# A Swin block and a dynamic convolution: scores on four 64x64 tiles, the first norm a round ahead on VectorE, activation tables called ahead, the end of the round reordered

## The chip, the cores and the metric

The kernel runs on one core of a Trainium2 chip, in one launch. The metric is the device time of that core in microseconds (us), as the median of several executions. All data are float32.

The engines that matter are TensorE (PE, with its weight loads shown apart as PEld), VectorE (DVE), ScalarE (ACT), GpSimd (POOL) and SyncE (SP, used here only to issue DMAs). Each works through its own instructions in program order and waits for others by semaphores.

## The reference, cut to what matters

The input x has 16 images of 192 channels and 56x56 pixels. Layer 0 is a Swin block with windows of 7x7, shifted by 3; layer 1 is a 3x3 depthwise convolution whose weights are computed from the image itself. The gains are ones and the biases zeros, but the kernel doesn't rely on that.

```python
h   = LN(x over channels) * g1 + b1; roll by (-3, -3); cut into 8x8 windows of 49 tokens
qkv = h @ qkv_w + qkv_b                      # 6 heads of 32
a   = softmax(q * 32**-0.5 @ k.T + rel_bias + shift_mask)
x1  = x + roll_back(concat(a @ v) @ proj_w + proj_b)
y   = x1 + gelu(LN(x1) @ fc1_w + fc1_b) @ fc2_w + fc2_b        # 192 -> 768 -> 192

t   = relu(bn(mean(y over pixels) @ w1.T))                     # 192 -> 48
wt  = (t @ w2.T + b2) with the taps behind the centre set to 0 # 4 of 9 are left
out = depthwise_conv3x3(y, wt) + bias
```

## The kernel before

**Tiling.** Channels lie on partitions. An image stays in SBUF in two tiles: x0 holds channels 0 to 127 of all rows, x1 the other 64 channels of the upper half on partitions 0 to 63 and of the lower half on 64 to 127. A step i handles two rows of windows, one of each half (h = 0, 1): T = 392 tokens each, 784 together. An image has four steps, so there are NS = 64 steps. Three images are in SBUF at a time.

**The main loop** (from L794) is a software pipeline. One round i works on several steps at once: the statistics of the first norm for step i+1, the attention of step i, the second norm of step i-1, the MLP of step i-2. The order of instructions on each engine is the order of the program (`manual_schedule`), so it is written out by hand:

1. `norm_stats` (L345): products with a selection matrix give means and mean squares in PSUM tiles `st`. `norm_devs` (L359): ACT squares the mean, DVE subtracts, ACT takes the square root (L371), DVE the reciprocal (L372). `norm_spread` (L376): 16 small DMAs from SP spread the rows of `dev` over all partitions (`dv`).
2. `mlp_first` (L651): six blocks `ph` of 128 hidden channels in three PSUM pairs. Blocks 0 to 2 are finished first, by `long` products (128 channels) and `short` ones (64). The short products of blocks 3 to 5 need the banks that the Gelu of blocks 0 to 2 (L663, ACT) empties.
3. `norm1_scale` (L388): GpSimd multiplies x by `dv` and writes the windows `win` of step i+1.
4. `attention_scores` (L527): for each of four pairs of windows (`wp`) eight products `sc`, then on DVE the bias `e` (L556), the maximum `top` (L562), its subtraction (L563), on ACT the exponential (L566), on DVE the sum `tot` (L570) and its reciprocal, on GpSimd the product `prob` (L572). These stages are interleaved over the four pairs.
5. `mlp_second` (L679): products `pf1`, then `pf` for the six blocks; behind blocks 2 to 5 stands a turn of the attention, six transposes `pt` (L593) and their copy `prt` by ACT (L599). The turns alternate between two pairs of PSUM banks, so the third needs the first one's copy done.
6. `mlp_out` (DVE), then on GpSimd `norm_squares` of step i+2 and `norm2_scale` of step i-1, then `attention_values` (`po`), the rest of two convolutions, `attention_qk` (`pq`, `pk`, `pe`), `project` (`pp`), `attention_v` (`pv`) and its copies.

In the scores before, a product contracts over 128 partitions: `kbd` holds the keys as a block diagonal, four heads of 32 wide with zeros elsewhere. One product of 196 columns makes the scores of four heads for one window, and one of 98 columns those of two. Two windows run side by side, since their outputs lie on different halves of the PSUM partitions.

**Convolution.** When the last step of an image is done, `taps_pool`, `taps_first` and `taps_second` compute the four taps. Then six pieces of the image go through `conv_begin` (ACT, L746, tile `y`) and `conv_rest` (DVE, three taps at L761, then the DMA out), two pieces in each of three rounds. DVE's taps stand ahead of its four copies of the keys into `kbd` (L460). At the end of the program the six pieces of the last image come one after the other.

**Activation tables.** ACT holds one set of functions; Sqrt, Gelu and Exp lie in three sets. The compiler puts an ACT_TABLE_LOAD right ahead of the first ACTIVATE that needs another set, so three to a round. Copies, Square, Identity and Relu cause none in the trace.

**Loading.** `load_x` (L91) is issued from ACT at the top of round 4b-2, five DMAs for image b.

Of the kernel before, what the change touches and what calls it, by code (L numbers as in the profile page):

```python
# [8 lines left out]
F32 = mybir.dt.float32  # L9
AF = mybir.ActivationFunctionType  # L10
# [26 lines left out]
def tile_swin_then_dynamic_conv(  # L37
# [199 lines left out]

    rel_r = work.tile([PW, N, HEADS], F32, tag="y", name="rel_r")
    nc.vector.memset(rel_r, 0.0)
# [4 lines left out]
    for j in range(2):  # L244
        for yq in range(WS):
# [8 lines left out]
            )  # L254
    bias_t = const.tile([PW, 2, 2, HEADS, N], F32, tag="bias_t", name="bias_t")
    rel_hk = rel_r[:, ::-1, :].rearrange("p k h -> p h k")
    for r in range(2):
        for e in range(2):
            cut = mask_t[:, r, e, :].rearrange("p (o k) -> p o k", o=1)
            nc.vector.tensor_tensor(  # L260
                bias_t[:, r, e], rel_hk, cut.broadcast_to([PW, HEADS, N]), ALU.add
            )

# [41 lines left out]

    kbd = one.tile([128, 3, NWIN, 4, N], F32, tag="kbd", name="kbd")
    vbd = const.tile([128, 2, NWIN, HEADS // 2, 64], F32, tag="vbd", name="vbd")
# [22 lines left out]

    sqs, stats = {}, {}

    def norm_squares(key, i, side, engine):
# [25 lines left out]
    def norm_devs(keys):  # L359


        sides = sorted(keys)
        d = one.tile([128, T], F32, tag="dev", name=f"dev_{keys[sides[0]]}")
        mean = {s: slice(s * 64, s * 64 + 64) for s in sides}
        var = {s: slice(64 - s * 64, 128 - s * 64) for s in sides}
        for s in sides:
            nc.scalar.activation(d[var[s]], stats[s][mean[s], :T], AF.Square)
        for s in sides:
            nc.vector.tensor_tensor(d[var[s]], stats[s][var[s], :T], d[var[s]], ALU.subtract)
        p = slice(0, 128) if len(sides) == 2 else var[sides[0]]  # L370
        nc.scalar.activation(d[p], d[p], AF.Sqrt, bias=eps_t[p])  # L371
        nc.vector.reciprocal(d[p], d[p])  # L372
        stats.clear()
        return d

    def norm_spread(keys, d):  # L376

        out = {}
        for side in sorted(keys):
            v = one.tile([128, 2, T], F32, tag=f"sq0{side}", name=f"dv_{keys[side]}")  # L380
            for h in range(2):
                at = 64 - side * 64 + h * 32
                for p in range(0, 128, 32):
                    nc.sync.dma_start(v[p : p + 32, h], d[at : at + 32])
            out[side] = v
        return out

    def norm1_scale(i, dv):  # L388
# [6 lines left out]
        for ws, cs, at, n in (  # L395
# [9 lines left out]
            for h in range(2):  # L405
                nc.gpsimd.tensor_tensor(  # L406
                    w0[:, h, :, ws, cs],
                    wide(v0[:, h]).rearrange("p r (w c) -> p r w c", w=n),
                    wide(b4[:, h]).rearrange("p r (w c) -> p r w c", w=n),
                    ALU.mult,  # L410
                )
            for h in range(2):
                p = slice(h * 64, h * 64 + 64)
                nc.gpsimd.tensor_tensor(
                    w1_[p, :, ws, cs],
# [26 lines left out]
    def attention_qk(i):  # L442
# [4 lines left out]
        ps, dsts = [], []  # L447
        for name, k in (("q", 1), ("k", 2), ("e", 0)):
            p = banks(f"p{name}_{i}", k)
            ps.append(p)  # L450
            dsts.append([p[:, h, :T].rearrange("p (w t) -> p w t", t=N) for h in range(2)])
        for m in range(3):
            long(dsts[m], wqkv, slice(m * 128, (m + 1) * 128), r0, True)
        for m in range(3):
            short(dsts[m], wqkv, slice(m * 128, (m + 1) * 128), r1, False)
        pq, pk, pe = ps
        nc.scalar.activation(q4, pq[:, :, :T], AF.Identity, bias=qkb[:, 0:1])
        for h in range(4):
            p = slice(h * HD, (h + 1) * HD)
            nc.vector.tensor_scalar(  # L460
                kbd[p, 0:2, :, h, :],
                pk[p, :, :T].rearrange("p h (w t) -> p h w t", t=N),
# [4 lines left out]
        for a in range(2):  # L467
# [3 lines left out]
            for h in range(2):  # L471
                p = slice(64 + h * HD, 64 + (h + 1) * HD)
                g = a * 2 + h
                nc.scalar.activation(
                    kbd[g * HD : (g + 1) * HD, 2, :, g, :],
                    pe[p, a, :T].rearrange("p (w t) -> p w t", t=N),
# [5 lines left out]
    def attention_v(i):  # L482
# [20 lines left out]

        whole(0, True)
        rest(0, False)
        rest(1, True)
        whole(1, False)
        return pvs
# [18 lines left out]
    def attention_scores(i, q4, q2):  # L527
# [5 lines left out]
        def add(wp):  # L533
            sc = banks(f"sc_{i}_{wp}", (1, 2, 0, 1)[wp])
            for g in range(4):
                a, heads = g % 2, slice(0, 4 * N) if g < 2 else slice(4 * N, 6 * N)
                for s in range(2):
                    w = wp * 2 + s
                    m = 64 - s * (64 - N)
                    cols = slice(w * N, w * N + m)  # L540
                    if g < 2:
                        lhs, rhs = q4[:, a, cols], kbd[:, a, w]
                    else:
                        lhs, rhs = q2[:, cols], kbd[:, 2, w, 2 * a : 2 * a + 2]
                    mm(
                        sc[s * 64 : s * 64 + m, a, heads],
                        lhs,
                        rhs.rearrange("p h t -> p (h t)"),
                        True,
                        True,  # L550
                    )
            e = one.tile([PW, 2, HEADS * N], F32, tag="e", name=f"e_{i}_{wp}", bufs=4)
            rel = bias_t[:, :, int(wp == 3)].rearrange("p r h k -> p r (h k)")
            if not last:
                rel = rel[:, 0:1, :].broadcast_to([PW, 2, HEADS * N])
            nc.vector.tensor_tensor(e, sc[:PW, :, : HEADS * N], rel, ALU.add)  # L556
# [45 lines left out]
    def attention_weigh(po, po1, wp, prt):  # L602
        for s in range(2):
            w = wp * 2 + s
            for a, g in ((0, 0), (0, 1), (1, 0), (1, 1), (0, 2), (1, 2)):
                o = po[:, a] if g < 2 else po1
                at = (g if g < 2 else a) * 64
                mm(
                    o[at : at + 64, w * N : (w + 1) * N],
                    vbd[:, a, w, g, :],  # L610
                    prt[:, a, g * PW + s * 64 : g * PW + s * 64 + N],
                    True,
# [16 lines left out]
    def project(i, o):  # L629
        pp1, pp = bank(f"pp1_{i}", 0), banks(f"pp_{i}", 1)  # L630
        for a in range(2):
            p = slice(a * 64, a * 64 + 64)
            mm(pp[:, a, :T], wp1[p], o[p, 2], True, False)
        for a in range(2):
            mm(pp1[a * 64 : a * 64 + 64, :T], wp0[:, C0:DIM], o[:, a], True, False)
        mm(pp1[:, :T], wp2, o[:, 2], False, True)
        for a in range(2):
            mm(pp[:, a, :T], wp0[:, 0:C0], o[:, a], False, True)
        v0, v1 = rows_of(i)
# [102 lines left out]
    def conv_begin(b, wt, n):  # L742

        kc, lo = (0, n * PR) if n < 4 else (1, (n - 4) * PR)
        y = work.tile([128, PR, IMG], F32, tag="y", name=f"y_{b}_{n}")
        nc.scalar.activation(  # L746
# [39 lines left out]

    yns, convs, qs = {}, [], {}
    ctx.enter_context(tc.manual_schedule())

    def has(i):  # L790
        return 0 <= i < NS

    norm_squares("1_0", 0, 0, nc.gpsimd)
    for i in range(-1, NS + 2):  # L794
        if (i + 2) % STEPS == 0 and 0 < (i + 2) // STEPS < B:
            b = (i + 2) // STEPS
            images[b] = load_x(b, nc.scalar)
        keys = {}
        if has(i + 1):
            keys[0] = f"1_{i + 1}"  # L800
            norm_stats(keys[0], i + 1, 0)
        if has(i - 1):
            keys[1] = f"2_{i - 1}"
            norm_stats(keys[1], i - 1, 1)
        dvs = norm_spread(keys, norm_devs(keys)) if keys else {}

        taps = convs[-1] if convs and "pooled" in convs[-1] else None

        def first_tap():
            if taps:  # L810
                taps["tt"] = taps_first(taps["b"], taps.pop("pooled"))

        hid = None
        if has(i - 2):
            hid = one.tile([128, NFC, 2, T], F32, tag="hid", name=f"hid_{i - 2}")
            mlp_first(i - 2, yns.pop(i - 2), hid, first_tap)
        else:
            first_tap()
        if 0 in keys:
            norm1_scale(i + 1, dvs[0])  # L820
        if has(i):
            attention_scores(i, *qs.pop(i))
        ys = []
        if convs and "wt" in convs[0]:
            c = convs[0]
            ys = [(c, c["n"] + k, conv_begin(c["b"], c["wt"], c["n"] + k)) for k in range(2)]
        prts = []
# [7 lines left out]
        else:  # L835
            for wp in range(4):
                turn(wp)
        if has(i + 2):
            norm_squares(f"1_{i + 2}", i + 2, 0, nc.gpsimd)
        if 1 in keys:  # L840
            yns[i - 1] = norm2_scale(i - 1, dvs[1])
        o = attention_values(i, prts) if has(i) else None
        for c, n, y in ys:
            conv_rest(c["b"], c["wt"], n, y)
            c["n"] = n + 1
            if n == 5:
                convs.pop(0)
        if has(i + 1):
# [89 lines left out]
```

## Time and profile before

| | |
|---|---|
| time | 3599.22 us, median of 3 (3596.49 to 3600.29) |
| profiled span | 3594.4 us |
| first statistics product | 56.2 us |
| PE work in the scores | 270.6 us (sc) |
| PE work in the MLP | 838.0 us (ph) and 814.9 us (pf) |
| ACT table loads in the loop | 191, of 1283 ns each |
| GpSimd on the first norm | 181.2 us (L406) and 183.9 us (L414) |
| DVE on the convolution's taps | 387.5 us (L761), 1358 ns each |

The busy time of a group is its own; engines work side by side, so the numbers don't add up to the span. The mean of one PE product includes its way through the array, so products that follow each other overlap, and the pace has to be read from several in a row. The program's time is told by the chain that ended last; a wait of an engine that isn't on it costs nothing. Since rounds repeat closely, a single round, read as a timeline, tells most of it.

### The profile page before, as it was taken

How to read it: one execution, taken by the hardware profiler on the slowest of the kernel's cores; microseconds unless marked ns; L12 is line 12 of the kernel's file. 1: busy time of each engine (PE TensorE's matmuls, PEld its weight loads, DVE VectorE, ACT ScalarE, POOL GpSimd, SP SyncE). 2: the span in 40 equal slices, each digit the busy share in tenths (PEclk: the TensorE clock that was granted, in tenths of full speed). 3: DMA queues.
4: the chain of work that ended last, by engine and by line, in shares of the span. 5: the costliest groups of instructions: out<-in, count | busy, mean ns of one | idle time of the engine just before them, and what ended most of it. 6: DMA issues, size and time to landing. Idle time of an engine off the chain costs nothing.

```text
span 3594.4 us, 62190 instructions
## 1 busy us (share of the span) xinstructions
PE 3394.8 (94%) x24854; PEld 2031.3 (57%) x24854; DVE 2120.9 (59%) x3309; ACT 1723.9 (48%) x2675; POOL 1119.3 (31%) x1374
## 2 busy tenths in 40 slices
PE   4699999999999999999999999999999999999996
PEld 2455655555555555555655555555655655555553
DVE  2554566665755756666665755656666565656654
ACT  0344455454545455445444545445445445545542
POOL 2332332332332332332332332332332332332320
PEclk8799999999999999999999999999999999999998
DMA  2010102001010111102001010111112011010101
GB/s 61 14 46 19 37 28 62 21 28 55 28 55 28 32 42 37 46 28 63 19 28 55 28 55 28 44 30 36 46 32 59 19 33 50 28 55 28 29 22 49
DMA packets 83074, 135.12 MB, mean 38 GB/s; under 512 B 25537, under 2 KB 65890, under 8 KB 80738
## 3 DMA queue, kind: packets, MB, share of 16 engines
q1 hardware_dynamic: 68384, 92.52, 9.1%
q10 hardware_dynamic: 14402, 38.64, 3.7%
q8 instruction: 196, 3.21, 0.4%
q14 instruction: 92, 0.75, 0.1%
HBM read 41.15 MB, written 38.54 MB: 22 GB/s over the span
## 4 chain that ended last, share of the span: by engine, by line
PE 72%; DVE 16%; ACT 6%; issue 3%; ACTq 1%; DMA 1%; POOL 0%; SPq 0%; DVEq 0%; POOLq 0%
PE pf L89 21%; PE ph L89 19%; DVE y L761 9%; PE pv L89 8%; PE sc L89 7%; DVE kbd L460 5%; PE st L89 4%; PE pt L593 4%; PE pp L89 2%; ACT L663 2%; PE po L89 2%; ACT hid L663 2%; PE pq L89 1%; PE pk L89 1%; PE pe L89 1%
## 5 line engine op out<-in xcount | busy, mean ns | idle before, releaser
L89 PE MATMUL ph<-yn,wf 128*128 128x392 f32 (+1 forms) x3072 | 838.0, 512 | 69.3 <-ACT hid L663 69.3
L89 PE MATMUL pf<-hid,wf 128*64 128x392 f32 (+1 forms) x3072 | 814.9, 495 | 0.0
L406 POOL TENSOR_TENSOR win<-x,dv 128x343 f32<-128x343 f32 (+2 forms) x384 | 181.2, 486 | 1810.4 <-DMA dv<-dev 1512.6
L89 PEld LDWEIGHTS ph<-yn,wf 128*128 128x128 f32 (+1 forms) x3072 | 407.9, 187 | 490.7 <-ACT hid L663 173.9
L89 PEld LDWEIGHTS pf<-hid,wf 128*64 128x64 f32 (+1 forms) x3072 | 377.1, 163 | 304.2 <-issue 128.5
L556 DVE TENSOR_TENSOR e<-sc,bias_t 113x588 f32<-113x588 f32 x256 | 195.9, 766 | 597.4 <-PE sc L89 497.3
L572 POOL TENSOR_TENSOR prob<-e,tot 113x588 f32<-113x588 f32 x256 | 294.9, 1174 | 526.1 <-DVE tot L571 524.3
L663 ACT ACTIVATE hid<-ph,f1b 128x784 f32<-128x784 f32 x384 | 337.2, 913 | 208.3 <-PE ph L89 207.5
L761 DVE SCALAR_TENSOR_TENSOR y<-x,wt,y 128x770 f32<-128x770 f32 x288 | 387.5, 1358 | 9.2 <-ACT y L746 2.4
L460 DVE TENSOR_SCALAR kbd<-pk,qkb 32x784 f32<-32x784 f32 x256 | 263.8, 1030 | 204.0 <-PE pk L89 201.1
L566 ACT ACTIVATE e<-e 113x588 f32<-113x588 f32 x256 | 177.5, 693 | 300.9 <-DVE e L563 300.4
L89 PE MATMUL pv<-wqkv,win 64*128 64x192 f32 (+1 forms) x2048 | 292.1, 338 | 18.5 <-DVE kbd L460 18.3
L89 PEld LDWEIGHTS pv<-wqkv,win 64*128 64x128 f32 (+1 forms) x2048 | 248.2, 190 | 81.2 <-PE pp L89 43.5
L89 PE MATMUL sc<-kbd,q 128*64 128x196 f32 (+3 forms) x4096 | 270.6, 289 | 6.1 <-DVE e L556 6.1
L599 ACT COPY prt<-pt 128x678 f32<-128x678 f32 x256 | 182.3, 722 | 191.0 <-PE pt L593 190.8
L89 PEld LDWEIGHTS sc<-kbd,q 128*64 128x64 f32 (+1 forms) x4096 | 233.6, 130 | 66.6 <-ACT hid L663 34.6
L89 PE MATMUL pp<-o,wp 128*128 128x392 f32 (+2 forms) x896 | 249.4, 512 | 1.4 <-ACT o L623 1.4
L523 DVE COPY vbd<-pv 49x192 f32<-49x192 f32 x512 | 159.5, 350 | 142.6 <-ACT vbd L525 97.5
L563 DVE TENSOR_TENSOR e<-e,top 113x588 f32<-113x588 f32 x256 | 233.0, 910 | 8.9
L593 PEld LDWEIGHTS pt<-ident,prob 113*128 113x128 f32 x1536 | 169.4, 143 | 118.3 <-POOL prob L572 56.9
L372 DVE RECIPROCAL dev<-dev 128x392 f32<-128x392 f32 (+1 forms) x66 | 171.8, 2603 | 84.5 <-ACT dev L371 84.5
L593 PE MATMUL pt<-ident,prob 113*128 113x113 f32 x1536 | 197.8, 266 | 23.7 <-POOL prob L572 23.7
(114 smaller groups left out, 4240.8 us busy)
## 6 DMA issues: line engine op xcount, KB each, us to landing
dv<-dev SPq DMA_DIRECT2D x1024, 49.0 KB
x<-in_x_dram ACTq DMA_DIRECT2D x15, 1484.0 KB
out_dram<-y SPq DMA_DIRECT2D x48, 392.0 KB
out_dram<-y SPq DMA_DIRECT2D x48, 196.0 KB
x<-in_x_dram ACTq DMA_DIRECT2D x15, 392.0 KB
x<-in_x_dram ACTq DMA_DIRECT2D x15, 350.0 KB
out_dram<-y SPq DMA_DIRECT2D x16, 308.0 KB
out_dram<-y SPq DMA_DIRECT2D x16, 154.0 KB
```

Of the source, the lines that this page charges most:

```text
L89: nc.tensor.matmul(dst, lhs, rhs, start=start, stop=stop, skip_group_check=True)
L372: nc.vector.reciprocal(d[p], d[p])
L406: nc.gpsimd.tensor_tensor(w0[:, h, :, ws, cs], wide(v0[:, h]).rearrange("p r (w c) -> p r w c", w=n), wide(b4[:, h]).rearrange("p r (w c) ...
L460: nc.vector.tensor_scalar(kbd[p, 0:2, :, h, :], pk[p, :, :T].rearrange("p h (w t) -> p h w t", t=N), qkb[p, 1:2], None, ALU.add,)
L556: nc.vector.tensor_tensor(e, sc[:PW, :, : HEADS * N], rel, ALU.add)
L563: nc.vector.tensor_tensor(ehs[wp], ehs[wp], t.broadcast_to([PW, 2 * HEADS, N]), ALU.subtract)
L566: nc.scalar.activation(es[wp], es[wp], AF.Exp)
L572: nc.gpsimd.tensor_tensor(prob[wp][:PW, :, 0:N], ehs[wp], t.broadcast_to([PW, 2 * HEADS, N]), ALU.mult)
L593: nc.tensor.transpose(pt[:, a, g * PW : (g + 1) * PW], prob[wp][:PW, h : h + 2, :].rearrange("p h k -> p (h k)"), ident[:PW, :PW],)
L599: nc.scalar.copy(prt, pt[:, :, : 3 * PW])
L663: nc.scalar.activation(hid[:, f], phs[f][:, :, :T], AF.Gelu, bias=f1b[:, f : f + 1])
L761: nc.vector.scalar_tensor_tensor(dst, src, wt[:, kc, t : t + 1], dst, ALU.mult, ALU.add)
```

## The change

Four things are changed together.

- **Scores.** A product now contracts over 64 partitions, two heads wide (`kbd` has two heads side by side instead of four), and its 64 outputs lie on one half of the PSUM partitions. So it takes a 64x64 quarter of the array; four run side by side, of the two halves of partitions (r) and two windows (s). There are twelve products of 98 columns for a pair of windows. The two row halves write to different PSUM banks. The order of heads in `e`, `prob` and `bias_t` follows.
- **First norm.** Its statistics are taken for step i+2 and scaled one round later, for step i+1, on VectorE right behind the reciprocal. The loop starts a round earlier. `dv` of this side gets a tile of its own.
- **Tables.** A one-element ACTIVATE (`table`) calls for Gelu behind the square root, for Exp behind the first layer, for Sqrt behind the scores, so that the load stands there.
- **Order.** Convolutions run three to a round in two rounds instead of two in three, one of them inside `mlp_first`; `y` gets three buffers. The second norm goes ahead of the squares on GpSimd; keys are computed ahead of queries, and `project` and `attention_v` take their products in another order. Images are loaded from SP a round earlier.

```diff
-    bias_t = const.tile([PW, 2, 2, HEADS, N], F32, ...)       # 4 additions
+    bias_t = const.tile([PW, 2, 2, 2, HEADS * N], F32, ...)   # 24 additions of two heads
...
-    kbd = one.tile([128, 3, NWIN, 4, N], F32, tag="kbd", name="kbd")
+    kbd = one.tile([128, 3, NWIN, 2, N], F32, tag="kbd", name="kbd")
...
+    def table(func):
+        nc.scalar.activation(junk, eps_t[0:1], func)
...
         nc.scalar.activation(d[p], d[p], AF.Sqrt, bias=eps_t[p])
+        table(AF.Gelu)
         nc.vector.reciprocal(d[p], d[p])
...
-        for side in sorted(keys):
-            v = one.tile([128, 2, T], F32, tag=f"sq0{side}", name=f"dv_{keys[side]}")
+        for side in sorted(keys, reverse=True):
+            tag = ("dv1", "sq01")[side]
+            v = one.tile([128, 2, T], F32, tag=tag, name=f"dv_{keys[side]}")
...
-                nc.gpsimd.tensor_tensor(          # norm1_scale, both loops
+                nc.vector.tensor_tensor(
...
-        for name, k in (("q", 1), ("k", 2), ("e", 0)):        # attention_qk
+        for name, k in (("k", 2), ("q", 1), ("e", 0)):
...
-        whole(0, True)                                        # attention_v
-        rest(0, False)
+        rest(0, True)
         rest(1, True)
+        whole(0, False)
         whole(1, False)
...
-            for g in range(4):                                # attention_scores
-                a, heads = g % 2, slice(0, 4 * N) if g < 2 else slice(4 * N, 6 * N)
-                for s in range(2):
-                    ...
-                    if g < 2:
-                        lhs, rhs = q4[:, a, cols], kbd[:, a, w]
-                    else:
-                        lhs, rhs = q2[:, cols], kbd[:, 2, w, 2 * a : 2 * a + 2]
-                    mm(sc[s * 64 : s * 64 + m, a, heads], lhs, rhs, True, True)
+            for g in range(3):
+                for r in range(2):
+                    p = slice(r * 64, r * 64 + 64)
+                    for s in range(2):
+                        ...
+                        mm(
+                            sc[s * 64 : s * 64 + m, r, g * 2 * N : (g + 1) * 2 * N],
+                            q4[p, g, cols] if g < 2 else q2[p, cols],
+                            kbd[p, g, w].rearrange("p h t -> p (h t)"),
+                            True,
+                            True,
+                        )
...
         for a in range(2):                                    # project
-            p = slice(a * 64, a * 64 + 64)
-            mm(pp[:, a, :T], wp1[p], o[p, 2], True, False)
-        for a in range(2):
             mm(pp1[a * 64 : a * 64 + 64, :T], wp0[:, C0:DIM], o[:, a], True, False)
         mm(pp1[:, :T], wp2, o[:, 2], False, True)
         for a in range(2):
-            mm(pp[:, a, :T], wp0[:, 0:C0], o[:, a], False, True)
+            mm(pp[:, a, :T], wp0[:, 0:C0], o[:, a], True, False)
+        for a in range(2):
+            p = slice(a * 64, a * 64 + 64)
+            mm(pp[:, a, :T], wp1[p], o[p, 2], False, True)
...
-        y = work.tile([128, PR, IMG], F32, tag="y", name=f"y_{b}_{n}")
+        y = work.tile([128, PR, IMG], F32, tag="y", name=f"y_{b}_{n}", bufs=3)
...
-    for i in range(-1, NS + 2):
-        if (i + 2) % STEPS == 0 and 0 < (i + 2) // STEPS < B:
-            images[b] = load_x(b, nc.scalar)
+    for i in range(-2, NS + 2):
...
-        if has(i + 1):
-            norm_stats(keys[0], i + 1, 0)
+        if has(i + 2):
+            norm_stats(keys[0], i + 2, 0)
...
-        dvs = norm_spread(keys, norm_devs(keys)) if keys else {}
+        dev = norm_devs(keys) if keys else None
+        if has(i + 1):
+            norm1_scale(i + 1, dvs.pop(0))
+        if keys:
+            dvs.update(norm_spread(keys, dev))
+        if (i + 3) % STEPS == 0 and 0 < (i + 3) // STEPS < B:
+            images[b] = load_x(b, nc.sync)
...
-        def first_tap():
+        def between():
             if taps:
                 taps["tt"] = taps_first(taps["b"], taps.pop("pooled"))
+            for b, wt, n in conv_ready(1):
+                conv_rest(b, wt, n, conv_begin(b, wt, n))
...
-        if 0 in keys:
-            norm1_scale(i + 1, dvs[0])
         if has(i):
+            table(AF.Exp)
             attention_scores(i, *qs.pop(i))
-        ys = []
-        if convs and "wt" in convs[0]:
-            ys = [(c, c["n"] + k, conv_begin(...)) for k in range(2)]
+        table(AF.Sqrt)
+        ys = [(*c, conv_begin(*c)) for c in conv_ready(2)]
...
-        if has(i + 2):
-            norm_squares(f"1_{i + 2}", i + 2, 0, nc.gpsimd)
         if 1 in keys:
-            yns[i - 1] = norm2_scale(i - 1, dvs[1])
+            yns[i - 1] = norm2_scale(i - 1, dvs.pop(1))
+        if has(i + 3):
+            norm_squares(f"1_{i + 3}", i + 3, 0, nc.gpsimd)
```

## The prediction

> **What bounds the kernel now.** I read the page first: the busy shares, then the chain that ended last.
>
> ```profile
> PE 3394.8 (94%) x24854; PEld 2031.3 (57%) x24854; DVE 2120.9 (59%) x3309; ACT 1723.9 (48%) x2675; POOL 1119.3 (31%) x1374
> ...
> PE 72%; DVE 16%; ACT 6%; issue 3%; ACTq 1%; DMA 1%; POOL 0%; SPq 0%; DVEq 0%; POOLq 0%
> ```
>
> TensorE (PE) is nearly always busy. Then I looked at single rounds of the main loop (one round is one pass over i, from its first statistics product to the next) by the windows table. Columns: length, busy time of PE, PE weight loads, VectorE (DVE), ScalarE (ACT), GpSimd (POOL), granted clock, DMA share, GB/s.
>
> ```profile
> 1522.77:1575.94 53.17, 51.92 (x384) 30.74 (x383) 34.64 (x51) 27.18 (x42) 17.82 (x21) 1.00 0.10 31
> ...
> 1682.85:1737.70 54.85, 53.69 (x403) 32.94 (x402) 27.44 (x50) 25.90 (x42) 17.03 (x21) 1.00 0.20 60
> 287.50:340.50 53.00, 51.90 (x383) 30.75 (x382) 26.59 (x46) 25.53 (x40) 16.10 (x21) 1.00 0.06 17
> ```
>
> A plain round takes 53.0 us, a round with convolutions 53.2 to 53.5, a round that computes taps 54.8; PE idles only 1.1 to 1.5 us of each. So a change pays only where it removes PE work or one of these few waits. Where they lie is told by the chain in order of time (start, length, what):
>
> ```profile
> 1578.78 5.06 PE ph L89 x16
> ...
> 1583.90 1.28 ACT L663
> ...
> 1586.16 6.69 PE ph L89 x24
> 1592.85 4.15 PE sc L89 x63
> 1597.00 8.10 PE pf L89 x36
> 1605.10 0.58 PE pt L593 x6
> ```
>
> The one PE wait in every round is in the first MLP layer: the Gelu table is loaded (1.28 us) only when the first block stands ready, and PE wants that bank back. The last view is the timeline after the scores, a round earlier (start, length, instruction, idle time before it and who ended it):
>
> ```profile
> 1540.94 0.77 DVE L556 TENSOR_TENSOR e<-sc,bias_t 113x588 f32<-113x588 f32 x1 [9.94 <-PE sc L89]
> ...
> 1549.62 1.17 POOL L572 TENSOR_TENSOR prob<-e,tot 113x588 f32<-113x588 f32 x1 [5.33 <-DVE tot L571]
> ...
> 1551.51 0.69 ACT L566 ACTIVATE e<-e 113x588 f32<-113x588 f32 x1 [2.21 <-DVE e L563]
> ...
> 1552.11 1.96 ACT L746 ACTIVATE y<-x,cb,wt 128x784 f32<-128x784 f32 x2
> ...
> 1552.50 3.43 POOL L572 TENSOR_TENSOR prob<-e,tot 113x588 f32<-113x588 f32 x3 [1.71 <-DVE tot L571]
> ...
> 1553.72 0.59 PEld L593 LDWEIGHTS pt<-ident,prob 113*128 113x128 f32 x6 [0.52 <-POOL prob L572]
> 1553.97 1.37 ACT L599 COPY prt<-pt 128x678 f32<-128x678 f32 x2
> ```
>
> The reader is to see that the softmax chain (DVE, then POOL) has no slack: the second set of transposes `pt` starts at 1553.72, just when the second `prob` is done (1552.50 plus a third of 3.43). PE has only just got there itself.
>
> [...] Before has no 64x64 form; it has four 32-column tiles (`st`), whose four products start within 0.02 us of each other (1522.76 to 1522.78)[...]. [...] The trace has 1283 for each of 191 loads; [...] (a load starts at 1526.45, where the ACTIVATE before ended at 1526.43). I take 1.28. [...] `e - top` (L563) takes 0.77 us, but 1.31 at 1550.11, under `prob`.
>
> **The change, part by part.**
>
> *Gelu table called after the square root.* ACT is idle 2.36 us before the late load, so the early one is hidden. The first Gelu then runs 1530.74 to 1531.65; PE has its own work until 1531.76, then the short products of blocks 3 to 5 follow at the pace of the three Gelus (2.53 us in all, 0.81 apart), and the long ones start near 1534.1 instead of 1535.46. About 1.35 us per round on PE, 63 rounds (63 loads at L663): **-85 us**. The Exp table called ahead gives nothing: the first Exp (1545.57) is not read until the `tot` of 1548.43.
>
> *Scores on four tiles.* One pass of 392 columns takes 0.33 us (`pf`: 36 instructions, 24 of them in pairs, so 24 slots in 8.10). Before: per window pair four slots of 196 columns and four of 98, 0.99 us, four times 3.96; measured 4.15. After: six slots of 98 on four tiles, 0.5 us, four times 2.0, with entry 2.2. Weight loads don't bind: `po` makes 96 instructions in 2.94 us on two tiles, 0.061 per slot, under 0.083. The bounds: 4.15 if tiles don't overlap by rows, 2.94 at `po`'s pace, 2.2 if free. I take 2.2: **-1.95 us on PE**. But behind it is the softmax. Its first add starts when the first pair is scored, 0.84 instead of 1.33 us into the scores, the second directly behind (1.53 instead of 2.34). So the chain moves by 0.8 us only, PE by 1.95, and PE waits some 0.25 us at the first transposes and 0.9 at the second. Net -0.8 us.
>
> *Square-root table called after the scores.* ACT runs it behind the last Exp: 1.28 plus a one-element ACTIVATE (0.29, as L297's). In a plain round the copy of the first transposes has room. In a convolution round two `y` (1.96) follow it before that copy: last Exp ends 11.8 us into the scores, table to 13.4, `y` to 15.3, copy to 16.05. The third transposes, for the same bank, could start at 15.2: PE waits 0.9. So a convolution round gets -0.8+0.9, nothing. Of 61 full rounds 28 will have convolutions (two in four instead of three in four, from the eighth on): 33 x -0.8 + 28 x 0.1 = **-24 us**.
>
> *First norm on VectorE, a round ahead.* Per round twelve instructions. By L556 (588 elements 0.77) four of 343 elements at 0.51 and eight small at 0.18: 3.5 us. They stand behind the reciprocal, where DVE idles 9.94 us before the first add (8.5 with the scores earlier). In a convolution round the new `between` adds three taps of 1.03: 6.6 of 8.5. Queued behind are the score additions; they don't wait. POOL loses 5.7 us that nobody waited for, so nothing gained.
>
> *Convolutions and the end of the round.* Before, DVE's six taps held back `kbd` (L460), so that PE waited about 0.2, 0.4 and 0.4 us at `pv` in three rounds of four. Now two of four; and POOL, still working when the taps start, ends nearer to them: about **-8 us**. The order of k, q and of `project` saves no instruction and as many changes of tile shape (each about 0.1 us). Loading x from SP frees ACT of some 3 us in 15 rounds, which delayed the Gelu in a few: **-3**.
>
> *Ends.* In the last round no convolution stands before the pooled sum (six taps, 3557.2 to 3563.4): -6; a third `y` buffer takes waits of 0.2 to 0.5 us from the last six: -1. At the start 24 bias additions for 4 (2.35 us; about 0.27 each) stand before what PE needs: +4; the extra round costs about +2.5. Sum **0**.
>
> Sum: -85 -24 -8 -3 = -120, **3480 us**.
>
> **Rivals.** *The whole scores saving lands*: if the probabilities came sooner than I think (no collision with POOL, quicker adds), each round keeps 1.95 and the table hides: -85 -119 -11 gives 3385. Against it: the twelve DVE instructions between the scores and `prob` run without a gap.
> *Row tiles don't overlap*, or the adds come late: only the Gelu and the small items remain, less 25 us for the square-root table: 3530.
> *VectorE becomes the bound*: if the norm's instructions with their 7-element runs took twice as long (7 us), convolution rounds would start the additions 2 us late, and if POOL's work also fell on the taps, 2 more; with scores that save nothing and 0.9 for the table, 28 rounds lose 4.9 and the 33 others 2 us, less Gelu's 85, plus 7 at the ends: 3599+137+66-85+7 = 3724. It speaks against it that DVE copies with short runs (L523, 192 elements in 0.35) are at the normal rate.
>
> **Chances.** Forecast 0.62, whole saving 0.12, no overlap 0.19, VectorE 0.07. The range leaves out VectorE and most of the whole saving: 3425 to 3545. Faster 0.92 (all but VectorE and a rest), same 0.02, slower 0.06.
>
> **What would show it.** Right: no table load before the first `hid`; `sc` near 2.2 us per round; PE waiting for `prob` at the second transposes about 0.9 us; for `prt` in convolution rounds; plain rounds near 51. Wrong: `sc` near 3 or 4; `e` waiting for DVE's own queue; `hid` still behind a table.

## The result and the profile after

The changed kernel takes **3443.49 us** (median of 4 runs, 3443.09 to 3443.57), against 3597.92 us for the kernel before beside it (3596.49 to 3600.29). The ratio is 0.957, with a 95% interval of 0.9553 to 0.9587. The prediction had said 3480 us, so 120 us less; it became 154 us less.

The page of the kernel after, first the busy shares, then the chain that ended last by engine:

```profile
PE 3270.0 (95%) x26902; PEld 1937.9 (56%) x26902; DVE 2259.6 (66%) x4098; ACT 1765.9 (51%) x2884; POOL 734.6 (21%) x606
...
PE 71%; DVE 18%; ACT 4%; issue 4%; POOL 1%; DMA 0%; ACTq 0%; SPq 0%; DVEq 0%; POOLq 0%
```

PE is busy 125 us less, although it issues 2048 products more (64 steps of 96 instead of 64): the smaller products run beside each other (in the plain round below they start in fours, each four within 0.02 us, most fours 0.084 us after the one before). With the first norm DVE has gained 139 us and POOL has lost 385. PE is still the bound.

Three rounds of the kernel after in the windows table (length, then busy time of PE, PE weight loads, DVE, ACT, POOL, then granted clock, DMA share, GB/s): a plain round, one with convolutions, one with taps.

```profile
1572.10:1622.70 50.60, 49.84 (x415) 29.34 (x414) 29.43 (x57) 25.91 (x44) 10.89 (x10) 1.00 0.22 65
1675.20:1726.40 51.20, 50.05 (x415) 29.26 (x414) 40.10 (x66) 28.63 (x47) 12.02 (x9) 1.00 0.13 41
1622.70:1675.20 52.50, 51.73 (x435) 31.51 (x434) 30.05 (x61) 26.22 (x45) 10.71 (x9) 1.00 0.07 17
```

A plain round has lost 2.4 us (53.0 to 50.6), and a round with taps 2.3 (54.8 to 52.5). Over the 60 rounds from the fourth to the last full one that makes 143.5 of the 154 us; the ends are looked at below.

Where it came from is told by the groups of PE (busy time and mean of one in ns, then the idle time ahead of it, with its releasers). First some rows of the kernel before, then the same of the kernel after:

```profile
L89 PE MATMUL ph<-yn,wf 128*128 128x392 f32 (+1 forms) x3072 | 838.0, 512 | 69.3 <-ACT hid L663 69.3
L89 PE MATMUL pv<-wqkv,win 64*128 64x192 f32 (+1 forms) x2048 | 292.1, 338 | 18.5 <-DVE kbd L460 18.3
L89 PE MATMUL sc<-kbd,q 128*64 128x196 f32 (+3 forms) x4096 | 270.6, 289 | 6.1 <-DVE e L556 6.1
L593 PE MATMUL pt<-ident,prob 113*128 113x113 f32 x1536 | 197.8, 266 | 23.7 <-POOL prob L572 23.7
```

```profile
L89 PE MATMUL ph<-yn,wf 128*128 128x392 f32 (+1 forms) x3072 | 819.2, 508 | 1.1 <-ACT hid L679 1.1
L89 PE MATMUL pv<-wqkv,win 64*128 64x192 f32 (+1 forms) x2048 | 275.8, 330 | 3.1 <-DVE kbd L477 3.1
L607 PE MATMUL pt<-ident,prob 113*128 113x113 f32 x1536 | 199.0, 267 | 76.7 <-POOL prob L586 65.4 <-ACT prt L613 11.2
L89 PE MATMUL sc<-kbd,q 64*64 64x98 f32 (+1 forms) x6144 | 156.7, 251 | 15.5 <-DVE e L570 15.1 <-ACT vbd L542 0.5
```

Four things are to be seen. The wait for `hid` is gone (69.3 to 1.1), and `ph` itself is 19 us shorter. The scores have lost 114 us. The transposes now wait 53 us more, 42 of them for `prob` and 11 for the copy `prt`: the softmax chain takes back a good part of what the scores gave. And `pv` has lost 16 us of its busy time and 15 of waits, more than was forecast for it.

The chain of the plain round in order of time (start, length, what), kernel after, shows the new wait:

```profile
1574.96 12.71 PE ph L89 x48
...
1598.62 0.69 DVE tot L584
...
1599.73 1.18 POOL prob L586
...
1614.84 3.84 PE pp L89 x14
1618.68 4.10 PE pv L89 x32
```

`ph` runs 48 products in one piece (before, it was cut by the table load). From 1588.5 to 1601 the chain lies on DVE and then POOL, not on PE: the second transposes start when the second `prob` is done. The timeline of the same round (start, length, instruction, idle time before it and who ended it) has the sizes:

```profile
1577.69 1.28 ACT L345 ACT_TABLE_LOAD   x1
1578.99 0.20 ACT L345 ACTIVATE junk<-eps_t 1x1 f32<-1x1 f32 x1
...
1580.02 2.53 ACT L679 ACTIVATE hid<-ph,f1b 128x784 f32<-128x784 f32 x3 [0.83 <-PE ph L89]
...
1587.60 2.43 PE L89 MATMUL sc<-kbd,q 64*64 64x98 f32 x96
...
1600.96 0.80 PE L607 MATMUL pt<-ident,prob 113*128 113x113 f32 x6 [0.77 <-POOL prob L586]
```

The scores in the same view of the kernel before:

```profile
1539.61 4.22 PE L89 MATMUL sc<-kbd,q 128*64 128x196 f32 x64
```

The Gelu table is loaded, its one-element ACTIVATE done, and ACT still waits 0.83 us for the first block. The 96 products of the scores take 2.43 us, where 64 took 4.22. PE waits once in this round, 0.77 us at the second `pt`.

### The profile page after: what moved, and what is told of

Read it like the earlier page. It is cut to its first block, busy times and chain, and to the rows that moved or that the text cites. A ratio compares the mean times of both kernels' runs of the same rounds, so it can differ in the third digit from the quotient of the medians.

```text
span 3441.8 us, 65409 instructions
## 1 busy us (share of the span) xinstructions
PE 3270.0 (95%) x26902; PEld 1937.9 (56%) x26902; DVE 2259.6 (66%) x4098; ACT 1765.9 (51%) x2884; POOL 734.6 (21%) x606
## 4 chain that ended last, share of the span: by engine, by line
PE 71%; DVE 18%; ACT 4%; issue 4%; POOL 1%; DMA 0%; ACTq 0%; SPq 0%; DVEq 0%; POOLq 0%
PE ph L89 24%; PE pv L89 8%; PE pp L89 7%; PE po L89 6%; DVE e L570 5%; PE st L89 5%; DVE top L576 5%; PE pk L89 4%; PE pf L89 4%; DVE e L577 4%; PE pq L89 4%; PE pe L89 4%; PE pt L607 3%; DVE tot L584 2%; ACT y L762 2%
## 5 line engine op out<-in xcount | busy, mean ns | idle before, releaser
L89 PE MATMUL ph<-yn,wf 128*128 128x392 f32 (+1 forms) x3072 | 819.2, 508 | 1.1 <-ACT hid L679 1.1
L777 DVE SCALAR_TENSOR_TENSOR y<-x,wt,y 128x770 f32<-128x770 f32 x288 | 342.6, 1199 | 23.8 <-ACT y L762 17.0
L89 PE MATMUL pv<-wqkv,win 64*128 64x192 f32 (+1 forms) x2048 | 275.8, 330 | 3.1 <-DVE kbd L477 3.1
L607 PEld LDWEIGHTS pt<-ident,prob 113*128 113x128 f32 x1536 | 162.4, 143 | 190.6 <-POOL prob L586 159.1
L724 DVE SCALAR_TENSOR_TENSOR x<-pf,f2b,x 128x784 f32<-128x784 f32 x64 | 66.2, 1034 | 230.6 <-PE pf L89 230.6
L542 ACT COPY vbd<-pv 49x192 f32<-49x192 f32 x512 | 135.4, 312 | 147.3 <-DVE vbd L540 147.3
L474 ACT ACTIVATE q<-pq,qkb 128x784 f32<-128x784 f32 x64 | 58.6, 916 | 290.3 <-PE pq L89 290.3
```

The source lines that it names most:

```text
L89: nc.tensor.matmul(dst, lhs, rhs, start=start, stop=stop, skip_group_check=True)
L607: nc.tensor.transpose(pt[:, a, g * PW : (g + 1) * PW], prob[wp][:PW, h : h + 2, :].rearrange("p h k -> p (h k)"), ident[:PW, :PW],)
L777: nc.vector.scalar_tensor_tensor(dst, src, wt[:, kc, t : t + 1], dst, ALU.mult, ALU.add)
```

## The experiments

**Theory:** three waits make up the result. The table load was PE's one wait in every round; the scores' saving is cut to 0.8 us by the softmax chain behind them; and the keys' copies held `pv` in more rounds than the profile showed, so that the new order at the end of the round counts. **Rivals:** the order is of no account and one of the first two is larger than thought; the table ahead works alone, without the load moved to SP; the first norm on VectorE helps or hurts somewhere. Each ratio below is to the kernel before beside it on the same chip. The kernel after did not run beside these, so a difference of a few us to it is also read from the rounds of the traces.

### The Gelu table ahead, alone

```diff
 # kernel before
         nc.scalar.activation(d[p], d[p], AF.Sqrt, bias=eps_t[p])
+        table(AF.Gelu)
```

> The kernel before, with nothing but the one-element Gelu behind the square root, so that the Gelu table stands ready. If the wait in the first layer is what the table costs, and nothing else takes its place: 63 rounds x 1.35 us off 3598, 3513 us. If PE, coming earlier, only waits longer for the second transposes (the softmax chain does not start earlier relative to the scores, but the scores do too, so this should not be): 3560 or more.

Measured: 3540.26 us, ratio 0.9848 (0.9833 to 0.9862), 56 us faster, and not the 85 forecast. A plain round and a convolution round lose 1.28 us each, near the forecast. The 15 rounds that load an image gain nothing (54.8 us before in the mean, 55.4 here). The chain of such a round, with this edit (ACTq is ACT's own queue):

```profile
602.19 0.33 ACTq L95
...
604.01 0.47 ACTq L98
...
604.53 0.49 ACT dev L371
...
607.50 1.28 ACT L335
...
609.01 0.92 ACT hid L668
```

The five DMA issues of `load_x` (2.34 us) stand on ACT ahead of the square, its square root and the Gelu table. So the table ends at 608.8, and the first Gelu runs behind it as before. That move of the load to SP was priced at 3 us: on its own, without the early table, that may be so (it was not run), but 15 rounds' worth of the Gelu gain depends on it. The converse is tried next.

### The load issued from ACT again, in the kernel after

```diff
 # kernel after, at the top of the round
+            images[b] = load_x(b, nc.scalar)
...
-            images[b] = load_x(b, nc.sync)
```

> The kernel after, with the images loaded from ScalarE at the top of the round, as before (still a round earlier). If its five DMA issues (2.3 us) push the square root and the Gelu table back until the first layer waits again, in the 15 rounds that load: 15 x 1.3 to 2 us, 3463 to 3473 us. If they are hidden: 3443 us.

Measured: 3473.61 us, ratio 0.9657 (0.9641 to 0.9672), 30 us slower than the kernel after. A load round takes 52.3 us in the mean instead of 50.59. The chain of one:

```profile
557.93 0.92 ACT hid L679
...
558.90 4.38 PE ph L89 x17
```

The first Gelu waits for the table, which runs from 556.41 to 557.69, and PE for that Gelu; PE idles 1.5 us ahead of `ph`. So the pair, table ahead and load on SP, is worth some 56 + 30 = 86 us (one step measured from the kernel before, the other from the kernel after), and the prediction's 85 + 3 = 88 was right for both together, with the shares wrong.

### The four 64x64 tiles, alone

```diff
 # kernel before: kbd two heads wide, twelve products of 98 columns, the order of bias_t and prt
-            for g in range(4):
+            for g in range(3):
+                for r in range(2):
...
-                    prt[:, a, g * PW + s * 64 : g * PW + s * 64 + N],
+                    prt[:, r, k * PW + s * 64 : k * PW + s * 64 + N],
```

> The kernel before, with nothing but the scores on four 64x64 tiles (with the layout of keys, bias and weighing that belongs to them). If the softmax chain eats the rest of the saving: 61 rounds x 0.8 us, 3549 us, and a new wait of about 0.8 us ahead of the second transposes. If the whole 1.8 us per round lands on the time: 3488 us. If row tiles did not overlap: 3598 us.

Measured: 3554.19 us, ratio 0.9887 (0.9872 to 0.9902), 42 us faster. A plain round loses 0.79 us: the scores take 2.36 instead of 4.15 us per round, so -1.79 (-1.70 from start to start), and the second transposes then start 0.84 us later than before, 0.74 of it shown as a wait. So the tiles do overlap, and the whole saving doesn't land; both rivals fall. Who waited for `prob` in this kernel, with time and times:

```profile
  PE pt L597: 70.5, 67
```

That is one wait in every round, with or without the other three changes.

### The old order of `project` and `attention_v`

```diff
 # kernel after
+            p = slice(a * 64, a * 64 + 64)
+            mm(pp[:, a, :T], wp1[p], o[p, 2], True, False)
...
-        rest(0, True)
+        whole(0, True)
+        rest(0, False)
```

> The kernel after, with the old order of products in project and attention_v. If this order is of no account, as the prediction had it: 3443 us. If it is what took 0.27 us of pp and pv work and the hold of pv by the keys off each round: 3443 + 61 x 0.3 to 0.5, that is 3462 to 3474 us.

Measured: 3472.62 us, ratio 0.9658 (0.9642 to 0.9674): 29 us slower than the kernel after, 0.62 us in every round without taps and 0.10 in those with taps. The timeline of that kernel:

```profile
540.82 3.91 PE L89 MATMUL pp<-o,wp 64*128 64x392 f32 x14 [0.36 <-ACT q L474]
...
544.56 4.46 PE L89 MATMUL pv<-wqkv,win 128*128 128x192 f32 x32
```

`pp` starts with the bank that ACT's copy of q empties, and with keys first that copy is the late one: 0.36 us of wait, and `pv` is longer too. With the new order of `project` the product into another bank goes first.

### The old order of keys and queries

```diff
 # kernel after
-        for name, k in (("k", 2), ("q", 1), ("e", 0)):
+        for name, k in (("q", 1), ("k", 2), ("e", 0)):
```

> The kernel after, with queries ahead of keys again. If the keys' copies, 0.66 us later, then hold back pv: up to 0.2 to 0.6 us a round, 3455 to 3480 us. If the order in project and attention_v alone made pv free: 3443 us.

Measured: 3448.07 us, ratio 0.9591 (0.9576 to 0.9605), 4.6 us slower: `pv` takes 4.23 us instead of 4.10. The intervals of the two ratios overlap, but every round without taps is 0.13 us longer in the trace, 5.8 us over the 60 rounds.

### Both old orders

```diff
 # kernel after: both edits above
```

> The kernel after, with the old order in project and attention_v and queries ahead of keys: the whole old end of the round, but for the convolutions. If pv is held by the keys' copies in every round (0.24 to 0.27 us in plain ones, as a longer pv rather than as idle time), and by 0.5 or more where convolution taps stand ahead of the keys: 3443 + 33 x 0.27 + 28 x 0.5, 3466 us. If the hold was only that of the convolution rounds before, and three in a round end no later than two: 3443 to 3450 us.

Measured: 3458.05 us, ratio 0.9617 (0.96 to 0.9634), 14.6 us slower than the kernel after. Each round, the plain ones too, is 0.3 us longer (those with taps 0.1). So the order does count, although it saves no instruction. Why can be read in the timeline of this kernel, here in a convolution round:

```profile
536.65 4.17 DVE L477 TENSOR_SCALAR kbd<-pk,qkb 32x784 f32<-32x784 f32 x4
...
540.97 4.54 PE L89 MATMUL pv<-wqkv,win 128*128 128x192 f32 x32
```

The last `pk` product ends at 536.60 and DVE's taps at 536.66, so the four key copies end at 540.82; `pv` follows 0.15 us later and takes 4.54 us. A plain round of the kernel before has the same end. Its chain, and then the keys in its timeline:

```profile
332.37 3.68 PE pp L89 x14
...
336.08 4.54 PE pv L89 x32
```

```profile
331.76 4.17 DVE L460 TENSOR_SCALAR kbd<-pk,qkb 32x784 f32<-32x784 f32 x4 [8.15 <-PE pk L89]
```

There too `pv` starts 0.15 us after DVE's last key copy (335.93), in step with `pp`'s modelled end. Its first products go to the PSUM banks of `pk`, which those copies empty. No idle time is shown, yet `pp` and `pv` together take 8.22 us, where they take 7.94 in the kernel after. The starts of single products in a plain round show the hold. With both old orders the first `pv` starts 0.56 us after the last `pp`, where the `pp` before it stand 0.33 us apart, and the second `pv` 0.24 us after the first, where the next ones stand 0.16 apart: 0.23 + 0.07 = 0.30 us, the whole difference of the round. In the kernel after the keys are done 0.78 us before `pv`. Most of the hold lies under the modelled end of the product before it: in that round of the kernel before, the last `pp` starts at 335.55 and is drawn 0.49 us long, and the first `pv` starts 0.53 us after it, at 336.08.

### The square-root table behind the turns

```diff
 # kernel after
-        table(AF.Sqrt)
         ys = [(*c, conv_begin(*c)) for c in conv_ready(2)]
...
             mlp_out(i - 2, *mlp_second(i - 2, hid, turn))
...
+        table(AF.Sqrt)
```

> The kernel after, with the call for the Sqrt table moved behind the four turns (transposes and copies). If the table and the two y stand in the way of the first copy, and so of the third transposes, in 28 convolution rounds by 0.58 us: 3443 - 16 = 3427 us. If that wait is made by the two y alone: 3443 us.

Measured: 3438.63 us, ratio 0.9562 (0.9547 to 0.9576), only 5 us better than the kernel after (4.9 us over the 60 rounds of the trace). What the load costs there is plain in the chain of a convolution round of the kernel after:

```profile
1702.48 1.28 ACT L345
...
1703.98 1.86 ACT y L762 x2
1705.84 0.61 ACT prt L613
...
1706.59 0.77 PE pt L607 x6
```

That wait of the third transposes is gone when the table goes behind. But another takes its place. The chain with the late table:

```profile
534.12 1.02 DVE y L777
535.14 0.93 DVE kbd L477
...
539.27 4.37 PE pv L89 x32
```

PE gets to `pv` sooner, DVE's taps and keys do not: `pv` is held again. Convolution rounds take 50.88 and 51.11 us, against 51.16.

### Two shares first, and the three moves together

The second pair's sum and `prob` (`share(1)`) stand behind the maximum of the fourth pair, and that makes the wait of every round. Put ahead of it, alone:

```diff
 # kernel after, attention_scores
+        share(1)
         top(3)
-        for wp in range(1, 4):
+        for wp in range(2, 4):
             share(wp)
```

> The kernel after, with the sums of the second pair (share 1) taken ahead of the maximum of the fourth (top 3) on VectorE. If the second probabilities, which come 2 us earlier, are what PE waits for (0.77 us in each of 61 rounds): plain rounds 0.7 us shorter, but in convolution rounds the last Exp, the Sqrt table and the two y come about 1 us later and hold the third transposes for it, so -0.7 x 33 and +0.5 to +1 x 28: about 3435 us. If PE waits for something else: 3443 us or slower.

Measured: 3508.08 us, ratio 0.9756 (0.974 to 0.9773): 65 us slower than the kernel after. Plain rounds hardly move (50.43: the wait goes to the third transposes). Of the 28 convolution rounds 21 take 53.9 to 54.0 us and 7 take 52.3. Windows of one of each, and the chain of the first:

```profile
442.00:496.00 54.00, 51.50 (x415) 30.19 (x414) 39.03 (x66) 28.61 (x47) 10.68 (x9) 0.97 0.12 38
652.70:705.00 52.30, 49.80 (x418) 29.34 (x417) 39.83 (x66) 28.59 (x47) 11.39 (x9) 1.00 0.12 39
```

```profile
470.41 1.28 ACT L345
...
471.91 1.86 ACT y L763 x2
473.77 0.61 ACT prt L614
...
474.52 0.77 PE pt L608 x6
475.29 2.48 PE pf L89 x4
477.77 1.11 PE pt L608 x6
```

The first two turns come sooner, and then PE idles 2.5 us for ACT (Exp, table, two `y`, copy). After that wait four `pf` take 2.48 us and six `pt` 1.11, where the same work takes 1.33 and 0.58 in the kernel after: the clock is at 0.97 for that round, and a further 1.7 us go there. In the 7 shorter rounds PE waits the same 2.5 us, and the clock stays at 1.00. So of the 65 us some 35 (21 times 1.7) are the clock. The new order of shares is thus only of use when ACT's queue is cleared too:

```diff
 # kernel after, all three
+        share(1)                       # ahead of top(3)
...
+        ys = [(*c, conv_begin(*c)) for c in conv_ready(2)]    # ahead of the scores
...
+        table(AF.Sqrt)                 # behind the turns
```

> The kernel after, with share 1 ahead of top 3, the Sqrt table behind the turns and the two y ahead of the scores on ScalarE. If both waits at the transposes (0.77 us in 61 rounds, 0.58 in 28) fall away: 3443 - 47 - 16 = 3380 us. If a later set of transposes then waits as long: 3443 us.

Measured: **3402.87 us**, ratio 0.9463 (0.9449 to 0.9477), 41 us better than the kernel after. A plain round takes 49.80 us and has no idle time of PE in it; convolution rounds take 50.56 and 50.79, with 0.49 and 0.74 us of wait for the keys at `pv`. What waiting is left has gone from POOL and ACT to DVE, and lies in convolution rounds alone.

### The first norm on GpSimd again

```diff
 # kernel after, norm1_scale, two places
-                nc.vector.tensor_tensor(
+                nc.gpsimd.tensor_tensor(
```

> The kernel after, with the first norm's scaling back on GpSimd (still a round ahead). If moving it was worth nothing, as predicted: 3443 us. If VectorE's 3 us stand in the way of the convolution taps and the scores: faster. If GpSimd's 5.7 us delay the probabilities or collide with VectorE's taps and subtractions: slower, by up to 0.5 us a round, 3475 us.

Measured: 3431.48 us, ratio 0.9542 (0.9528 to 0.9556), 12 us better than the kernel after. In the full rounds it makes no difference (50.56 against 50.59), as the prediction said. The gain is at the start. The first three rounds in the windows table, here and in the kernel after:

```profile
57.50:177.10 119.60, 76.86 (x713) 50.14 (x715) 61.22 (x92) 53.84 (x94) 38.45 (x56) 0.79 0.14 38
```

```profile
58.20:187.70 129.50, 77.49 (x713) 51.51 (x712) 70.12 (x128) 53.87 (x94) 22.14 (x19) 0.75 0.13 35
```

While no MLP runs yet, nothing covers the norm's instructions on DVE, and the first additions of the scores queue behind them. The wait of `sc` for `e` in the groups shows 6 of these 10 us: 15.1 us in the kernel after, 8.8 here (6.1 before). The first wait of `pk` for `win` shows 3 more, 14.1 against 11.1.

### The best version, and one more move

```diff
 # the three moves, with norm1_scale on GpSimd
```

> Share 1 ahead of top 3, the Sqrt table behind the turns, the two y ahead of the scores (as in the three moves, 3403), and the first norm's scaling on GpSimd (as in that run, 10 us shorter at the start). If the two add up: 3392 us. If GpSimd's 5.7 us, ahead of the earlier second probabilities, hold them: 3403 us or more.

Measured: **3392.97 us** (3391.05 to 3393.44), ratio 0.9433 (0.9418 to 0.9448), faster than both kernels. The gains nearly add up: 41 and 12 apart, 51 together. A plain round in the windows table:

```profile
530.10:579.90 49.80, 49.80 (x417) 29.36 (x416) 26.86 (x45) 25.84 (x44) 16.25 (x23) 1.00 0.24 66
```

PE is busy for all of its 49.80 us. What is left is the hold in the convolution rounds, so two of three convolutions were put into `mlp_first`:

```diff
 # the best version
-            for b, wt, n in conv_ready(1):
+            for b, wt, n in conv_ready(2):
...
-        ys = [(*c, conv_begin(*c)) for c in conv_ready(2)]
+        ys = [(*c, conv_begin(*c)) for c in conv_ready(1)]
```

> The one before, with two of the three convolutions of a round inside the first layer and one behind the attention. If the taps ahead of the keys' copies are what holds pv (0.49 and 0.74 us in convolution rounds, and a restart of 0.27): 28 x 0.8 to 1.0 less, 3366 us. If VectorE's six taps then end after the first scores (6.3 us against about 5 of idle time), the scores' additions and all transposes start up to 1.5 us late: 3392 us or more.

Measured: 3402.50 us, ratio 0.946 (0.9445 to 0.9475), 10 us worse than the best version. The timeline of a convolution round:

```profile
445.56 1.44 DVE L570 TENSOR_TENSOR e<-sc,bias_t 113x588 f32<-113x588 f32 x2
446.38 0.73 PE L89 MATMUL sc<-kbd,q 64*64 64x98 f32 x24 [1.01 <-DVE e L570]
```

The hold at `pv` is gone; but DVE's taps are still running when the scores stand ready, the first addition is late, and the fourth pair of scores wants its bank: 1.0 us of wait here, 1.2 in the other convolution round of an image. DVE is busy for some 39 of 50.5 us in such a round of the best version, but its idle time does not lie where the taps can go.

## Why the prediction came out as it did

Its forecast was the mechanism that happened; the sum came out 34 us small. The signs of being right that it named are all there: no table load ahead of the first `hid`, 2.36 us of scores per round, PE waiting 0.77 us for `prob` at the second transposes and 0.38 for `prt` in convolution rounds, plain rounds of 50.6 us. By its steps:

- **Gelu table, -85, and the load, -3: right as a pair.** The first experiment and the load from ACT give -56 and -30. Over the 60 rounds, idle time ahead of `ph` fell by 66 us and `ph` by 18: 1.4 us per round, where 1.35 was worked out. The step in it that failed is "Loading x from SP frees ACT of some 3 us in 15 rounds, which delayed the Gelu in a few": it delayed the Gelu in every load round, and its price was a third of the Gelu's.
- **Scores, 2.2 us and a wait of 0.9: right.** Measured 2.36 us and 0.77 per round. "Net -0.8" became -0.79 in a plain round of the experiment with the tiles alone. The four 64x64 tiles run side by side: 96 products of 98 columns took 2.36 us, against 4.15 for the 64 longer ones. "Before has no 64x64 form" holds for the loop only: ahead of it stand ten products of that shape, of one column each.
- **Square-root table, 0.9 in a convolution round: too large by 9 us.** The wait was 0.38 us, 0.57 with the 0.19 that PE loses on starting again (six `pt` in 0.77 us instead of 0.58), over 28 rounds. Two terms were too large: the one-element ACTIVATE takes 0.20 us, not 0.29, and the two `y` (1.96 us, as assumed) start 0.1 us before it ends, where they were put behind it. That is 0.19 of the 0.33 us per round; the rest was not taken apart. Without the wait only 5 us came back, since `pv` waits in its place.
- **Convolutions and the end of the round, -8: the step that failed.** It became about -30 over the 60 rounds: waits ahead of `pv` -15, `pv` itself -23, `pp` +8 (counting only the time after the end of the product before). "The order of k, q and of `project` saves no instruction and as many changes of tile shape" is true, and the conclusion that it therefore gives nothing is not. The hold by the keys was in the plain rounds too, not only in the three of four with convolutions. No idle time showed it; that `pp` followed by `pv` took 8.22 us did. 14.6 us of the 30 are the order by itself (both old orders). The other 15 or so are left for the convolutions' new places and for GpSimd's new order, which were not run apart.
- **First norm on VectorE, "nothing gained": right for the rounds** (it takes 3.0 us of DVE; 3.5 was worked out), and not at the start, where it costs 10 us.
- **Ends, 0: nearly.** The first statistics product comes 2.0 us later and the first three rounds take 4.1 more: 6.1, where 6.5 was worked out. The last round fell from 92.4 to 82.8 us, 9.6 where 7 was worked out: the wait ahead of the pooled product went from 7.5 to 1.3 us. Of the 3 us more than forecast 1.6 are the clock: the 16 products `w` behind that wait took 3.57 us at a granted clock of 0.50 before, and take 1.94 at 1.00 after.

The excess of 34 us is thus 22 at the end of the round, 9 at the square-root table and 3 at the tail. Of the rivals, "the whole scores saving lands" (3385) is the one that the best version comes near to, at 3393, but only by moving four other things: it is not what this change did. The steps run apart give 86 (table and load), 42 (tiles), 15 (order) and -12 (first norm): 131 of the 154 us. The remaining 23 lie in what was not run apart and in how the parts act on each other. "VectorE becomes the bound" did not come, but the experiment with two convolutions inside the first layer shows it begin, 1.0 to 1.2 us at a time.

## What to carry to other kernels

A wait that the profile shows as idle is a lower bound: a hold can be covered by the modelled end of the product before it (here 0.30 us a round with no idle time shown). So compare the starts of the same products in kernels that are held and kernels that are not. When a wait is taken away, the next engine in the order takes its place (here, once POOL's `prob` was out of the way, ACT's table and `y`, then DVE's keys, then DVE's additions), so queues are moved together, and one move alone can be a loss of 65 us where three are a gain of 41. And DMA issues on an engine's own queue count as its work (here 2.34 us of ACT for five): look for them ahead of whatever is being called early.

## What the runs showed of the hardware that had not been expected

- Four products of 98 columns on the four 64x64 tiles share one slot: in a plain round of the kernel after each four start within 0.02 us, most of them 0.084 us after the four before. 96 of them in 2.36 us are 24 slots of 0.098 us, near the 0.083 us that a quarter of a 392-column slot (0.33 us in `pf`) gives.
- A table load took 1.28 us and no more: in the plain round of the kernel after it starts 0.02 us after the square root's end (1577.67), and the next ACTIVATE starts 0.01 us after its own (1578.97). Calling it early costs 1.28 us and one ACTIVATE of 0.20 us on a 1x1 tile.
- With two shares first, 28 rounds had the same PE wait of 2.50 us. In 21 of them the products then ran at about half their pace for a while (four `pf` in 2.48 us instead of 1.33, six `pt` in 1.11 instead of 0.58; 1.7 us lost, mean granted clock of the round 0.97), in 7 they did not (1.00). What sets the 21 apart from the 7 was not shown. In the kernel after, with its waits of 0.77 us, the granted clock was 1.00 from the fourth round to the last full one.
